# The sum of a softmax taken from ScalarE's accumulator output instead of a VectorE reduction

## The chip, the cores and the metric

The kernel runs on one core of a Trainium2 chip, as one launch. The metric is the device time of the whole launch in microseconds (us). A core has five engines, each with a queue of its own that it works through in order: TensorE (PE in the profile, with PEld for its weight loads), VectorE (DVE), ScalarE (ACT), GpSimd (POOL) and SyncE (SP, which here only starts DMAs). They meet through semaphores. Matrix products are written to a memory of their own, PSUM, which PE fills and ACT and DVE read out.

## What is computed

The input x is 8 x 512 x 128 (batch, position, feature), in float32. A first block adds the layer-normed result of a causal linear attention. The second block, in which the change lies, is a transformer of six layers over the same 8 x 512 positions: each layer has an attention over windows of 32 positions with 16 heads of 64 features, and a feed-forward part with a gated GELU. The attention of a window, cut to what matters here:

```python
sim = jnp.einsum('bhwie,bhwje->bhwij', bq, bk2) * QK_SCALE   # 32 queries x 64 keys
sim = jnp.where(mask, -jnp.finfo(sim.dtype).max, sim)
attn = jax.nn.softmax(sim, -1)
out = jnp.einsum('bhwij,bhwje->bhwie', attn, bv2)
```

The 64 keys of a window are those of the window before it and its own. Each row's softmax needs the largest score, the exponentials, and the sum of the 64 exponentials.

## The kernel before

A unit of work is a tile of 128 positions (four windows) of one batch item in one layer: 6 layers x 8 items x 4 tiles j = 192 units. The loop over t at the end of `sandwich_kernel` takes the units as a pipeline written out by hand: at step t it projects unit t, turns the queries and keys of unit t-1 to features and forms its scores, weighs the values of unit t-2, and projects the output of unit t-3. After the fourth tile of an item come the feed-forward parts: `feed_norm`, `feed_first`, `feed_middle` and `feed_last`, in the steps after it.

The loop stands in a `manual_schedule` of PE alone: PE's instructions are issued in the order in which the program writes them. The order on ACT, DVE and POOL is worked out when the kernel is built, from dependencies and priorities; a block under `tc.high_priority()` goes ahead of other ready work, and `issue_behind` ties one instruction behind another on its engine (here, each exponential behind the table load that it needs: GELU uses another table than the exponential and logarithm, so ACT loads tables twice for each batch item of a layer).

What a step does around the change, in PE's order:

- `proj` (L421) makes q and then k of unit t, in a PSUM buffer "mm". DVE multiplies by the rotary tables (L429 twice, L436 once), ACT squares both halves (L444). Only after these is the buffer free. There are two "mm" buffers, for q, k and `values` (L481), so L481 takes the one that q had. DVE sums the squares (L457).
- Between q and k, `out_project` (L603) does its products for unit t-3, which DVE adds to the state (L608).
- `by_keys` (transposes at L70, in two halves of four) turns the exponentials of unit t-2 for use as weights; ACT copies each half to pT (L564).
- `values` (L481) and ACT's copy of them (L482, and two DMA shifts for windows) follow, then `by_features` (L70, copies at L514), `weigh_values` (L574) with DVE's division by the sum (L582), and `by_features` again.
- `scores` (L527 lays down the mask, L534 adds the products) fills a PSUM tile of 128 rows x 16 heads x 64 keys. DVE takes the negated maximum of each head (L542). ACT makes 16 exponentials (L546), one for each head, 64 elements wide on 128 partitions, since each has another maximum as its bias. DVE sums all 16 x 64 in one reduction (L552) and takes the reciprocal (L553).
- `out_by_features` (L70, copies to oT at L596) ends the step.

The reduction and the reciprocal write "su", a tile of 128 x 16, of which there are two, as there are of "pe", the exponentials.

Of the kernel before, what the change touches and what calls it, by code (L numbers as in the profile page):

```python
# [8 lines left out]
F32 = mybir.dt.float32  # L9
BF16 = mybir.dt.bfloat16  # L10
AF = mybir.ActivationFunctionType
ALU = mybir.AluOpType
AX = mybir.AxisListType
PSUM = bass.MemoryType.PSUM

P = 128
# [10 lines left out]
def sandwich_kernel(ctx: ExitStack, tc: tile.TileContext, ins: dict, out: bass.AP):  # L27
    nc = tc.nc
# [57 lines left out]
    def issue_behind(later, earlier):  # L86
        tc.add_manual_dep(
            later.ins, earlier.ins.name,
            mybir.DependencyInfo(mybir.DependencyClass.NoSync, mybir.DependencyReason.DATA),
            reason="order on an engine",  # L90
        )
# [30 lines left out]
    f2 = ctx.enter_context(tc.tile_pool(name="f2", bufs=2))  # L122
# [4 lines left out]
    NP = H // 2  # L127
# [391 lines left out]
    def scores(u):  # L519

        qT, kT = u["qT"], u["kT"]


        mk = mask0 if u["j"] == 0 else mask
        sp = psum.tile([P, 2, NP, 2 * W], F32, tag="s", name="sp", bufs=1)
        for p in range(2):
            nc.tensor.matmul(  # L527
                sp[:, p], identb, mk.unsqueeze(1).to_broadcast([P, NP, 2 * W]),
                start=True, stop=False, skip_group_check=True,
            )  # L530
        for pair in range(NP):
            for w in range(4):
                for p in range(2):
                    nc.tensor.matmul(  # L534
                        sp[W * w : W * (w + 1), p, pair, :],
                        qT[HD * p : HD * (p + 1), pair, W * w : W * (w + 1)],
                        kT[HD * p : HD * (p + 1), pair, W * w : W * (w + 2)],
                        start=False, stop=True, skip_group_check=True,
                    )
        mx = f2.tile([P, 2, NP], F32, tag="mx", name="mx")  # L540
        with tc.high_priority():
            nc.vector.tensor_reduce(mx, sp, AX.X, ALU.max, negate=True)  # L542
        pe = f2.tile([P, NP, 2, 2 * W], F32, tag="pe", name="pe")
        for pair in range(NP):
            for p in range(2):
                ex = nc.scalar.activation(  # L546
                    pe[:, pair, p, :], sp[:, p, pair, :], AF.Exp, bias=mx[:, p, pair : pair + 1]
                )
                issue_behind(ex, tables[-1])
        exps.append(ex)  # L550
        su = f2.tile([P, NP, 2], F32, tag="su", name="su")
        nc.vector.tensor_reduce(su, pe, AX.X, ALU.add)  # L552
        nc.vector.reciprocal(su, su)  # L553
        u["pe"], u["su"] = pe, su

# [138 lines left out]
    with tc.manual_schedule(engines={mybir.EngineType.PE}):  # L694
# [8 lines left out]
        for t in range(len(units) + 7):  # L703
# [31 lines left out]
            if gelus:  # L735
                at(t, 0, unit_length)
            at(t, 6, feed_last, ends=True)
            at(t, 1, scores)
            at(t, 2, out_by_features)

# [90 lines left out]
```

## Time and profile before

| | |
|---|---|
| median of 3 runs | 3899.76 us (3896.29 to 3900.25) |
| the profiled execution | 3893.85 us, of which its span is 3892.1 us |
| granted TensorE clock | 0.99 |
| mean of one exponential, L546 | 376 ns, 3072 of them, 651.4 us of ACT |
| mean of one sum, L552 | 1220 ns, 192 of them, 234.2 us of DVE |
| mean of one reciprocal, L553 | 243 ns, 192 of them |
| mean of one square, L444 | 610 ns, 768 of them |
| one maximum, L542 | 1222 ns, 192 of them |

The profile lists, for each group of instructions, its source line and engine, what it writes and reads ("pe<-sp,mx"), the shapes, how often it ran, its busy time in us and the mean of one in ns, and the idle time of the engine just before it with what ended that idle time. ACT's durations overlap: the next instruction starts before the one before has ended. In the timeline every row has its start, its length, the engine, the line, and in brackets the idle time ahead of it and the releaser. "issue" is time in which an engine waited for nothing that the profile shows. The chain is followed back from the last instruction of the program to what released each, so that its shares say where a shorter instruction would have brought the end nearer.

### The profile page before, as it was taken

The numbers are of one execution on the slowest core, as the hardware profiler recorded it, in microseconds if no ns is written. First come the engines' busy times: TensorE is split into PE (matmuls) and PEld (weight loads), VectorE is DVE, ScalarE is ACT, GpSimd is POOL, SyncE is SP. The second block draws the span as 40 slices with busy tenths as digits, with TensorE's granted clock in tenths as the row PEclk, the third lists the DMA queues.
The fourth block names the chain that finished last, engine by engine and source line by source line (L and its number), as shares of the span: only waits on it lengthen the run. The fifth ranks groups of instructions, "written<-read, shape, count | busy, mean of one in ns | idle before, by whom it ended". The sixth has DMA issues, their size and how long they took to land.

```text
span 3892.1 us, 149565 instructions
## 1 busy us (share of the span) xinstructions
PE 3729.8 (96%) x65600; PEld 2474.2 (64%) x65600; DVE 2818.2 (72%) x4300; ACT 2657.5 (68%) x6745; POOL 1837.0 (47%) x1311
## 2 busy tenths in 40 slices
PE   8999989999999999999999999999999999999997
PEld 4555456666666666666666666666666666666665
DVE  4555567777867777777777777777787777777775
ACT  5565656776767777777777677777677777766664
POOL 0000025555555555555555555555555555555552
PEclk9999999999999999999999999999999999999998
DMA  2000012222222222222222322223222222222221
GB/s 81 17 9 12 6 50 71 59 66 60 76 74 63 63 63 66 71 75 65 60 62 64 82 65 66 65 56 82 70 66 59 66 65 56 65 68 68 64 67 37
DMA packets 153208, 233.46 MB, mean 60 GB/s; under 512 B 32622, under 2 KB 53356, under 8 KB 151788
## 3 DMA queue, kind: packets, MB, share of 16 engines
q1 hardware_dynamic: 152556, 223.89, 22.4%
q8 instruction: 517, 8.47, 0.9%
q14 instruction: 135, 1.11, 0.1%
HBM read 24.54 MB, written 4.19 MB: 7 GB/s over the span
## 4 chain that ended last, share of the span: by engine, by line
PE 89%; ACT 5%; issue 3%; DVE 2%; DMA 0%; POOL 0%; POOLq 0%; DVEq 0%; SPq 0%; ACTq 0%
PE tr L70 17%; PE mm L421 17%; PE mm L481 9%; PE py L603 9%; PE sp L534 7%; PE po L574 6%; PE y L282 4%; PE mm L625 3%; PE py L657 3%; PE mm L626 3%; PE sc L252 2%; PE sp L527 2%; ACT sq L444 2%; PE vv L230 2%; PE po L318 2%
## 5 line engine op out<-in xcount | busy, mean ns | idle before, releaser
L454 POOL TENSOR_TENSOR qk<-t,t 128x1024 f32<-128x1024 f32 x384 | 909.2, 2368 | 999.6 <-DVE t L436 999.5
L421 PE MATMUL mm<-wqkv,state 128*128 128x512 f32 x1536 | 727.1, 596 | 3.7 <-ACT v L482 2.6
L470 POOL TENSOR_TENSOR qk<-qk,ss 128x1024 f32<-128x1024 f32 x384 | 722.3, 1902 | 16.0
L429 DVE TENSOR_TENSOR t<-mm,tab 128x512 f32<-128x512 f32 x768 | 497.8, 685 | 242.8 <-PE mm L421 231.3
L546 ACT ACTIVATE pe<-sp,mx 128x64 f32<-128x64 f32 x3072 | 651.4, 376 | 27.6 <-DVE mx L542 27.3
L436 DVE TENSOR_TENSOR t<-mm,tab 128x1024 f32<-128x1024 f32 x384 | 465.9, 1213 | 0.0
L457 DVE TENSOR_REDUCE ss<-sq 128x16 f32<-128x1024 f32 x384 | 461.9, 1203 | 2.0 <-ACT sq L444 2.0
L444 ACT ACTIVATE sq<-mm 128x512 f32<-128x512 f32 x768 | 422.6, 610 | 47.2 <-DVE t L436 45.6
L603 PEld LDWEIGHTS py<-oT,wo 128*128 128x128 f32 x3072 | 374.8, 193 | 93.5 <-issue 56.2
L70 PEld LDWEIGHTS tr<-ident,qk 128*128 128x128 f32 x3072 | 345.7, 141 | 127.1 <-issue 105.7
L70 PE MATMUL tr<-ident,qk 128*128 128x128 f32 x3072 | 412.1, 277 | 7.4 <-ACT qT L514 2.3
L596 ACT COPY oT<-tr 128x512 f32<-128x512 f32 x384 | 207.3, 589 | 266.2 <-PE tr L70 265.2
L421 PEld LDWEIGHTS mm<-wqkv,state 128*128 128x128 f32 x1536 | 264.1, 192 | 191.6 <-issue 188.0
L481 PE MATMUL mm<-wqkv,state 128*128 128x512 f32 x768 | 367.9, 602 | 16.8 <-ACT sq L444 16.8
L603 PE MATMUL py<-oT,wo 128*128 128x128 f32 x3072 | 376.0, 276 | 1.0 <-ACT oT L596 0.9
L582 DVE TENSOR_TENSOR on<-po,su 128x1024 f32<-128x1024 f32 x192 | 235.1, 1224 | 170.1 <-PE po L574 170.1
L534 PEld LDWEIGHTS sp<-kT,qT 64*32 64x32 f32 x24576 | 271.9, 106 | 116.7 <-issue 113.8
L574 PE MATMUL po<-v,pT 64*32 64x64 f32 x24576 | 299.3, 225 | 44.7 <-issue 44.7
L482 ACT COPY v<-mm 128x1024 f32<-128x1024 f32 x192 | 194.5, 1013 | 211.0 <-PE mm L481 211.0
L534 PE MATMUL sp<-kT,qT 64*32 64x64 f32 x24576 | 312.2, 227 | 26.0 <-issue 25.2
L574 PEld LDWEIGHTS po<-v,pT 64*32 64x32 f32 x24576 | 258.5, 105 | 86.4 <-issue 86.2
L542 DVE TENSOR_REDUCE mx<-sp 128x16 f32<-128x1024 f32 x192 | 234.6, 1222 | 106.9 <-PE sp L534 106.3
(108 smaller groups left out, 5171.0 us busy)
## 6 DMA issues: line engine op xcount, KB each, us to landing
v<-v SPq DMA_DIRECT2D x1152, 128.0 KB
v<-v SPq DMA_DIRECT2D x672, 64.0 KB
wqkv<-in_L_ffn_Wqkv_dram SPq DMA_DIRECT2D x6, 1536.0 KB
wo<-in_L_ffn_Wo_dram SPq DMA_DIRECT2D x6, 512.0 KB
xin<-_attn_hidden_states_dram SPq DMA_DIRECT2D x8, 256.0 KB
xr<-_attn_hidden_states_dram SPq DMA_DIRECT2D x8, 256.0 KB
x<-xr SPq DMA_DIRECT2D x8, 256.0 KB
xr<-x SPq DMA_DIRECT2D x8, 256.0 KB
```

Of the source, the lines that this page charges most:

```text
L70: nc.tensor.transpose(ps[:cols, :rows], src, ident[:rows, :rows])
L421: nc.tensor.matmul(ps[:, a].rearrange("p h d -> p (h d)"), lhs, wqkv[:, s, a, :], start=True, stop=True)
L429: nc.vector.tensor_tensor(t2[:, a], ps[:, 1 - a], tab[:, 2 * s + 1, j, HF * a : HF * (a + 1)].unsqueeze(1).to_broadcast([P, H, HF]), ALU.mult,
L436: nc.vector.tensor_tensor(t1, ps, tab[:, 2 * s, j, :].rearrange("p (a d) -> p a d", a=2).unsqueeze(2) .to_broadcast([P, 2, H, HF]), ALU.mult,)
L444: nc.scalar.activation(sq[:, :, a, :], ps[:, a], AF.Square)
L454: nc.gpsimd.tensor_tensor(qk[:, s].rearrange("p h a d -> p a h d"), t1, t2, ALU.add)
L470: nc.gpsimd.tensor_tensor(t, t, ss[:, i, :].unsqueeze(2).to_broadcast([P, H, HD]), ALU.mult)
L481: nc.tensor.matmul(ps[:, p, :], lhs, L["wqkv"][:, 2, p, :], start=True, stop=True)
L534: nc.tensor.matmul(sp[W * w : W * (w + 1), p, pair, :], qT[HD * p : HD * (p + 1), pair, W * w : W * (w + 1)], kT[HD * p : HD * (p + 1), pa ...
L546: ex = nc.scalar.activation(pe[:, pair, p, :], sp[:, p, pair, :], AF.Exp, bias=mx[:, p, pair : pair + 1])
L574: nc.tensor.matmul(po[W * w : W * (w + 1), p, pair, :], pT[r, pair, W * w : W * (w + 1)], v2[r, w, HD * pair : HD * (pair + 1)], start=Tru ...
L603: nc.tensor.matmul(py, L["wo"][:, c, :], oT[:, c, :], start=(c == 0), stop=(c == NP - 1))
```

## The change

Each of the 16 exponentials also writes the sum of what it has computed, into its own element of "su", by ACT's accumulator output. The tile "su" is therefore made ahead of the exponentials, and the reduction on DVE is gone. The reciprocal stays.

```diff
         pe = f2.tile([P, NP, 2, 2 * W], F32, tag="pe", name="pe")
+        su = f2.tile([P, NP, 2], F32, tag="su", name="su")
         for pair in range(NP):
             for p in range(2):
                 ex = nc.scalar.activation(
-                    pe[:, pair, p, :], sp[:, p, pair, :], AF.Exp, bias=mx[:, p, pair : pair + 1]
+                    pe[:, pair, p, :], sp[:, p, pair, :], AF.Exp, bias=mx[:, p, pair : pair + 1],
+                    accum_out=su[:, pair, p : p + 1],
                 )
                 issue_behind(ex, tables[-1])
         exps.append(ex)
-        su = f2.tile([P, NP, 2], F32, tag="su", name="su")
-        nc.vector.tensor_reduce(su, pe, AX.X, ALU.add)
         nc.vector.reciprocal(su, su)
         u["pe"], u["su"] = pe, su
```

## The prediction

> **What bounds the kernel now.** I read the page first (busy shares, the chain that ended last), then the costliest groups for the lines of the change, then who waits for the exponentials, then three stretches of the timeline.
>
> ```profile
> PE 3729.8 (96%) x65600; PEld 2474.2 (64%) x65600; DVE 2818.2 (72%) x4300; ACT 2657.5 (68%) x6745; POOL 1837.0 (47%) x1311
> ...
> PE 89%; ACT 5%; issue 3%; DVE 2%; DMA 0%; POOL 0%; POOLq 0%; DVEq 0%; SPq 0%; ACTq 0%
> ```
>
> PE works through its fixed order almost without a break, and 89% of the chain is PE. ACT is on the chain for 5%, DVE for 2%. So DVE time is worth little, and ACT time costs something wherever PE stands close behind ACT.
>
> ```profile
> L546 ACT ACTIVATE pe<-sp,mx 128x64 f32<-128x64 f32 x3072 | 651.4, 376 | 27.6 <-DVE mx L542 27.3
> ...
> L552 DVE TENSOR_REDUCE su<-pe 128x16 f32<-128x1024 f32 x192 | 234.2, 1220 | 9.5 <-ACT pe L546 3.5
> ...
> L553 DVE RECIPROCAL su<-su 128x16 f32<-128x16 f32 x192 | 46.6, 243 | 0.1
> ```
>
> These are the groups of the change: 16 exponentials, one sum and one reciprocal in each of 192 steps. The sum, 234.2 us of DVE, hardly ever waited for ACT (3.5 us).
>
> ```profile
> 2051.60 3.40 ACT L546 ACTIVATE pe<-sp,mx 128x64 f32<-128x64 f32 x16
> ...
> 2055.38 1.09 ACT L444 ACTIVATE sq<-mm 128x512 f32<-128x512 f32 x2 [0.39 <-DVE t L436]
> ...
> 2055.82 1.22 DVE L552 TENSOR_REDUCE su<-pe 128x16 f32<-128x1024 f32 x1
> ...
> 2056.74 1.08 ACT L564 COPY pT<-tr 128x512 f32<-128x512 f32 x2 [0.27 <-PE tr L70]
> 2056.87 0.30 PEld L481 LDWEIGHTS mm<-wqkv,state 128*128 128x128 f32 x2
> ...
> 2058.08 0.24 DVE L553 RECIPROCAL su<-su 128x16 f32<-128x16 f32 x1
> ...
> 2058.36 1.29 DVE L429 TENSOR_TENSOR t<-mm,tab 128x512 f32<-128x512 f32 x2
> ```
>
> An ordinary step in the timeline (start, length, engine). The exponentials end at 2055.00. Behind them in ACT's queue stand the two squares of q (L444), 1.09 us; when these are done, the "mm" buffer of q is free and PE may start the values (L481). ACT idled 0.39 us, and after the squares ended at 2056.47 another 0.40 passed until PE came, at 2056.87: 1.87 us from the last exponential to L481.
>
> ```profile
> 2030.48 3.39 ACT L546 ACTIVATE pe<-sp,mx 128x64 f32<-128x64 f32 x16
> ...
> 2033.89 1.28 ACT L82 ACT_TABLE_LOAD   x1
> ...
> 2035.19 1.09 ACT L444 ACTIVATE sq<-mm 128x512 f32<-128x512 f32 x2
> ...
> 2036.33 0.30 PEld L481 LDWEIGHTS mm<-wqkv,state 128*128 128x128 f32 x2 [0.55 <-ACT sq L444]
> ```
>
> A step with the GELU table: the load stands between, ACT has no gap, and PE's L481 already waits for ACT. Every ns more on ACT here is a ns of the end.
>
> ```profile
> 2698.66 3.38 ACT L546 ACTIVATE pe<-sp,mx 128x64 f32<-128x64 f32 x16 [0.64 <-DVE mx L542]
> 2701.82 1.21 ACT L444 ACTIVATE sq<-mm 128x512 f32<-128x512 f32 x2
> 2703.04 1.07 ACT L564 COPY pT<-tr 128x512 f32<-128x512 f32 x2
> ```
>
> A third kind: the exponentials waited for the maximum, the squares follow without a gap, and L481 starts at 2703.17, 1.13 us after the last exponential.
>
> **What the Trainium skill says.** "ScalarE: Activation LUTs", section What ACT_TABLE_LOAD costs, prices an ACTIVATE at 186 ns + 0.833 ns per element, 93 more for a pointer operand, with 93 of overlap back to back: for 64 elements and a pointer bias 333 ns alone, 240 in a row. The trace has 376 for one, and (3.38 - 0.376) / 15 = 200 from start to start; the page is off by some 40 each way. Its table load of 1283 ns agrees exactly. "ScalarE activation tables: per-element evaluation and per-set limits", section What a function is on this engine, says that the accumulator output adds the results along the free dimension, but not what reading it out costs. "VectorE: DVE Perf Modes", section Two Vector instructions with no wait between them, says of VectorE that an op which also writes out its accumulator is two instructions, the second a read of the accumulator. I expect the same of ACT; no run here shows it yet.
>
> **The change part by part.**
>
> *Removed:* 192 sums, 192 x 1.220 = 234 us of DVE. They lie between other DVE work while PE does L70 and L481. The reciprocal (0.24) stays and now needs only ACT; its result is used by L582, 3 us later. What is queued behind it on DVE is the k half's L429; should the reciprocal wait for a late last sum, L429 waits too, but it already starts at 2058.36 behind 1.22 us of work that is gone. With the sum gone, k's L429 and L436 can end 1.2 us sooner, and so k's squares. That helps where PE waits for a copy queued behind those squares: the transposes of xn waited 22.5 us for the qT copy (L514). Bounds: nothing, up to about 100 us (these 22.5 and DVE's 2% of the chain, 78). I take 15, two thirds of the 22.5, since L481 and other ACT work still stand in front.
>
> *Added:* 3072 accumulator reads. I estimate one at the page's price for a one-element ACTIVATE without pointer: 187 ns of record, less 93 of overlap, 94 in a row. Bounds: below, nothing (the sum is written by the exponential itself); above, no overlap at all, (376 + 187) - 200 = 363 ns. At 94 the exponentials of a step end X = 16 x 0.094 = 1.50 us later.
>
> *What hides X.* The soonest that L481 follows the last exponential is 1.05 us (two squares and a signal), or 2.45 with a table load. I took the real interval in every step of the timeline. By tile j of the exponentials the medians are 1.88, 1.16, 2.45 and 1.87 us; the mean slack, interval less soonest, is 0.84, 0.26, 0.04 and 0.82 us (j = 0 to 3). PE is in order, so what exceeds the slack delays everything behind L481, the next scores, maximum and exponentials included: it comes back in every step. Four steps: (1.50 - 0.84) + (1.50 - 0.26) + (1.50 - 0.04) + (1.50 - 0.82) = 4.04 us; times 48 such fours, 194 us. The transposes of pe (L70) have more room: each needs only two of the exponentials, and the eighth loads about 1.6 us after the last one ends.
>
> *Moved:* nothing by hand, but only PE's order is written out; ACT's is found at build time. The first step of the timeline shows what may happen when exponentials are late:
>
> ```profile
> 572.65 0.64 ACT L546 ACTIVATE pe<-sp,mx 128x64 f32<-128x64 f32 x2
> 573.06 0.72 ACT L444 ACTIVATE sq<-mm 128x512 f32<-128x512 f32 x1
> 573.71 0.58 ACT L564 COPY pT<-tr 128x512 f32<-128x512 f32 x1
> 574.20 0.60 ACT L444 ACTIVATE sq<-mm 128x512 f32<-128x512 f32 x1
> ...
> 574.85 0.50 PEld L481 LDWEIGHTS mm<-wqkv,state 128*128 128x128 f32 x2 [1.37 <-ACT sq L444]
> ```
>
> One pT copy came before the last two exponentials, the other between the squares, and L481 waited 1.37 us. A pT copy in front of the squares costs 0.49 us (start to start). Bounds: nothing to 192 x 0.49 = 94. I take half, 47. The stalls that the chain calls "issue" (3%, 117 us) could shrink while PE waits anyway; I take nothing for that.
>
> *Sum:* 194 + 47 - 15 = +226. On the span 3892.1 that gives 4118; the profiled execution took 3893.85, 1.75 more than its span, and the median of the runs shown, 3899.76, is 5.9 above that: 4126 us.
>
> **Rivals.**
>
> *The read doesn't overlap* (25%). If the record's whole 187 ns adds to each exponential, X = 3.0 and the step costs (12.0 - 1.96) x 48 = 482, some 4380 us; at 363 ns, X = 5.8 and 4920. For it: a read has to wait until the last element has come through. Against it: the exponentials themselves start 176 ns before their predecessors end.
>
> *The read is nearly free and hides in the slack* (10%). At 47 ns X = 0.75: only j = 1 and 2 pay, (0.49 + 0.71) x 48 = 58, less 15 of relief, about 3943.
>
> *DVE's relief wins* (10%): the other side. The accumulator comes with the ACTIVATE or within 20 ns of it, X is 0.3 at most and costs (0.04 + 0.26) x 48 = 14 us, while k's squares move up, PE meets them done at xn and elsewhere, and 15 to 100 us go: about 3870. It decides below 20 ns a read for the small relief, below about 60 ns (X = 1.0, 97 us) for the greatest. For it: DVE's 2% and ACT's 5% of the chain. Against it: the sum lay where PE was busy.
>
> *The change doesn't do what it says:* the sums could still be late for L582, as the reciprocal waits for the last read. L582 starts after PE's L574, 3 us on, so this costs nothing unless X passes 3; it is within the first rival.
>
> **How the numbers follow.** The forecast, reads of 60 to 140 ns, has 55% and reaches from about 4020 to 4270. The range 3940 to 4500 adds the small-cost case and that part of the first rival with reads up to some 215 ns (15 of its 25%); left out are the relief (10%) and reads above that (10%). What a measurement of this kernel tells from no change is 0.2%, 8 us. Faster: the relief rival less a little, 9%. Within 0.2%: 3%, from the border of the two cheap cases. Slower: 88%.
>
> **What would show it.** Right: ACT has 3072 more short records at L546, the exponentials of a step last 4.9 us instead of 3.39, ACT's busy share rises beyond 75%, DVE loses 234 us, and L481 waits for ACT sq L444 in all four kinds of step, with ACT's share of the chain well above 5%. Wrong: exponentials that still last 3.4 us, or a longer stretch that ends in no wait of PE.

## The result

The changed kernel takes 4153.5 us (median of 4 runs, 4148.75 to 4155.69) beside 3898.03 us for the kernel before on the same chip: a ratio of 1.0656, 95% interval 1.0637 to 1.0674. It is slower by 255 us. In the two profiled executions the span went from 3892.1 to 4153.8 us, 262 more.

The page of the changed kernel, busy shares and the chain that ended last:

```profile
PE 3823.4 (92%) x65600; PEld 2500.1 (60%) x65600; DVE 2607.5 (63%) x4108; ACT 2910.4 (70%) x9817; POOL 1843.5 (44%) x1311
...
PE 52%; ACT 39%; DVE 6%; issue 2%; DMA 0%; SPq 0%; POOL 0%; POOLq 0%; DVEq 0%; ACTq 0%
...
L547 ACT ACTIVATE pe<-sp,mx 128x64 f32<-128x64 f32 x3072 | 913.4, 364 | 22.4 <-DVE mx L542 21.8
L547 ACT ACTIVATION_READ_ACCUMULATOR pe<-sp,mx 128x1 f32 x3072 | 789.1, 258 | 0.0
```

ACT is busy for only 70% of the span, 68% before, and still it carries 39% of the chain, 5% before. DVE lost 211 us of busy time, and its share of the chain rose from 2% to 6%. What sets the end is how late ACT is at one place, not how full it is. The 3072 new rows are the accumulator reads; each stands in the trace for 258 ns on average.

The stretch behind the exponentials of an ordinary step, in the timeline of the changed kernel:

```profile
2104.93 0.41 ACT L547 ACTIVATE pe<-sp,mx 128x64 f32<-128x64 f32 x1
...
2105.22 0.42 ACT L547 ACTIVATE pe<-sp,mx 128x64 f32<-128x64 f32 x1
2105.41 0.32 ACT L547 ACTIVATION_READ_ACCUMULATOR pe<-sp,mx 128x1 f32 x1
2105.51 1.20 ACT L444 ACTIVATE sq<-mm 128x512 f32<-128x512 f32 x2
...
2106.75 0.30 PEld L481 LDWEIGHTS mm<-wqkv,state 128*128 128x128 f32 x2 [0.58 <-ACT sq L444]
```

From one exponential to the next it is now 0.29 us, 0.20 before: a read adds 0.09 us, though its own row lasts 0.21 to 0.32 in this step, since the rows overlap. The first exponential of this step starts at 2100.88, so all 16 take 4.85 us in place of 3.39. The squares (L444) follow without the gap of 0.39 us that stood there before, and the weight load of L481 waits for them.

The step with the GELU table is another matter. In the kernel before, ACT copied to pT behind the squares (those at 2035.19 in the prediction's second timeline):

```profile
2036.16 1.08 ACT L564 COPY pT<-tr 128x512 f32<-128x512 f32 x2
```

In the changed kernel, first ACT, then PE:

```profile
2007.31 1.28 ACT L82 ACT_TABLE_LOAD   x1
2008.60 1.07 ACT L564 COPY pT<-tr 128x512 f32<-128x512 f32 x2
2009.56 2.09 ACT L444 ACTIVATE sq<-mm 128x512 f32<-128x512 f32 x4
```

```profile
2010.72 3.00 PE L481 MATMUL mm<-wqkv,state 128*128 128x512 f32 x4 [2.74 <-ACT sq L444]
```

Both pT copies (L564) now stand ahead of the squares, and PE waits 2.74 us. Then something else happens: the four matmuls of L481 take 3.00 us, while they take 1.98 in the ordinary step. The view by stretches, whose seventh number (PEclk) is the granted TensorE clock:

```profile
2006.90:2010.70 3.80, 1.08 (x9) 0.80 (x7) 2.67 (x4) 3.77 (x10) 2.25 (x2) 1.00 0.00 0
2010.70:2014.70 4.00, 3.98 (x10) 2.24 (x11) 1.22 (x1) 1.89 (x4) 1.76 (x1) 0.61 0.00 0
```

(The numbers after the stretch are its length, the busy times of PE, PEld, DVE, ACT and POOL with their counts, the clock, and DMA.) After the stall PE got 0.61 of its clock for the 4 us that follow. In 29 of the 46 such steps that I compared, the way from L481 to L574 took 4.05 to 5.42 us; in the other 17 it took 2.79, as before.

The distance from the first exponential of a step to that of the next, averaged over the steps of each kind (j is the tile of the exponentials; worked out from the timelines, the first four steps left out), is the measure for all that follows. In us:

| | j = 0 | j = 1 | j = 2 (GELU) | j = 3 |
|---|---|---|---|---|
| before | 15.73 | 15.27 | 20.26 | 17.48 |
| changed | 16.36 | 16.48 | 23.30 | 18.06 |
| squares first | 16.32 | 16.39 | 21.58 | 18.13 |
| 8 reads, squares first | 15.71 | 15.70 | 20.94 | 17.49 |
| table load later | 16.35 | 16.49 | 20.29 | 18.11 |

The differences of the first two rows, 0.63 + 1.21 + 3.04 + 0.58 = 5.46 us, times 48 give 262 us: the whole of the span's growth.

### The profile page after: what moved, and what is told of

Read it like the earlier page. It is cut to its first block, busy times and chain, and to the rows that moved or that the text cites. A ratio compares the mean times of both kernels' runs of the same rounds, so it can differ in the third digit from the quotient of the medians.

```text
span 4153.8 us, 152353 instructions
## 1 busy us (share of the span) xinstructions
PE 3823.4 (92%) x65600; PEld 2500.1 (60%) x65600; DVE 2607.5 (63%) x4108; ACT 2910.4 (70%) x9817; POOL 1843.5 (44%) x1311
## 4 chain that ended last, share of the span: by engine, by line
PE 52%; ACT 39%; DVE 6%; issue 2%; DMA 0%; SPq 0%; POOL 0%; POOLq 0%; DVEq 0%; ACTq 0%
ACT pe L547 22%; PE mm L481 10%; PE tr L70 10%; PE po L574 6%; ACT sq L444 5%; PE sp L534 4%; ACT oT L596 4%; PE y L282 4%; PE mm L625 3%; PE py L657 3%; PE mm L626 3%; PE sc L252 2%; PE vv L230 1%; ACT L76 1%; PE po L318 1%
## 5 line engine op out<-in xcount | busy, mean ns | idle before, releaser
L454 POOL TENSOR_TENSOR qk<-t,t 128x1024 f32<-128x1024 f32 x384 | 907.7, 2364 | 875.5 <-DVE t L436 875.5
L547 ACT ACTIVATE pe<-sp,mx 128x64 f32<-128x64 f32 x3072 | 913.4, 364 | 22.4 <-DVE mx L542 21.8
L547 ACT ACTIVATION_READ_ACCUMULATOR pe<-sp,mx 128x1 f32 x3072 | 789.1, 258 | 0.0
L421 PE MATMUL mm<-wqkv,state 128*128 128x512 f32 x1536 | 727.3, 596 | 4.5 <-ACT v L482 2.6
L481 PE MATMUL mm<-wqkv,state 128*128 128x512 f32 x768 | 413.8, 665 | 187.0 <-ACT sq L444 187.0
L436 DVE TENSOR_TENSOR t<-mm,tab 128x1024 f32<-128x1024 f32 x384 | 465.9, 1213 | 0.0
L70 PEld LDWEIGHTS tr<-ident,qk 128*128 128x128 f32 x3072 | 361.6, 146 | 143.0 <-issue 117.6
L444 ACT ACTIVATE sq<-mm 128x512 f32<-128x512 f32 x768 | 433.1, 658 | 5.8 <-DVE t L436 5.7
L70 PE MATMUL tr<-ident,qk 128*128 128x128 f32 x3072 | 428.2, 284 | 7.4 <-issue 2.8
L421 PEld LDWEIGHTS mm<-wqkv,state 128*128 128x128 f32 x1536 | 263.8, 192 | 192.9 <-issue 189.3
L481 PEld LDWEIGHTS mm<-wqkv,state 128*128 128x128 f32 x768 | 136.2, 197 | 331.2 <-ACT sq L444 231.9
L574 PE MATMUL po<-v,pT 64*32 64x64 f32 x24576 | 298.4, 227 | 27.8 <-issue 27.6
```

The lines of the kernel that those rows point to most:

```text
L70: nc.tensor.transpose(ps[:cols, :rows], src, ident[:rows, :rows])
L421: nc.tensor.matmul(ps[:, a].rearrange("p h d -> p (h d)"), lhs, wqkv[:, s, a, :], start=True, stop=True)
L436: nc.vector.tensor_tensor(t1, ps, tab[:, 2 * s, j, :].rearrange("p (a d) -> p a d", a=2).unsqueeze(2) .to_broadcast([P, 2, H, HF]), ALU.mult,)
L444: nc.scalar.activation(sq[:, :, a, :], ps[:, a], AF.Square)
L454: nc.gpsimd.tensor_tensor(qk[:, s].rearrange("p h a d -> p a h d"), t1, t2, ALU.add)
L481: nc.tensor.matmul(ps[:, p, :], lhs, L["wqkv"][:, 2, p, :], start=True, stop=True)
```

## The experiments

The first four ran on one chip beside the kernel before at 3892.56 us, the next three beside 3897.68, then three beside 3889.11, the last beside 3891.57.

**The reads with the sum kept** (e1). The reads write to a spare tile; DVE sums as before.

```diff
-                    accum_out=su[:, pair, p : p + 1],
+                    accum_out=sx[:, pair, p : p + 1],
...
+        nc.vector.tensor_reduce(su, pe, AX.X, ALU.add)
         nc.vector.reciprocal(su, su)
```

> The reads go to a spare tile and DVE's sum is kept and used. If the whole loss is ACT's reads (my theory), the freed DVE time bought nothing and this takes what the changed kernel takes: 4153 us, give or take 10. If the freed DVE time paid part of the reads back (the relief of 15 to 100 us in the prediction), this is slower than the changed kernel by that much: 4170 to 4250.

Measured: 4151.8 us, a ratio of 1.067 (1.0645 to 1.0694). With 234 us more of DVE work it takes what the changed kernel takes: the two ratios to the kernel before, 1.067 and 1.0656, differ by less than either interval is wide. The loss is ACT's reads, and no part of them that could be measured is paid back by DVE's freed time.

**No sum and no reads** (e2 and e8). First the relief of DVE alone, with a `tensor_scalar` in place of sum and reciprocal:

```diff
-        nc.vector.tensor_reduce(su, pe, AX.X, ALU.add)
-        nc.vector.reciprocal(su, su)
+        nc.vector.tensor_scalar(su, pe[:, :, :, 0], 1.0, None, ALU.add)
```

> Left out: the sums altogether, by DVE and by ACT; the reciprocal is replaced by one DVE operation of the same size that adds 1 to the first exponential of each head, so it still waits for the exponentials. This is the relief of DVE alone. My theory: nothing, 3885 to 3900 us. The relief rival: 15 to 100 us below the kernel before, 3800 to 3883.

Measured: 3907.78 us, 1.0042 (1.0028 to 1.0057), 0.4% slower than before. The experiment was not what I meant it to be. By the view of the tile su, the stand-in was longer than the sum and the reciprocal together, 1.46 us, that it replaced (shortest, median and longest in ns):

```profile
L552 DVE TENSOR_SCALAR su<-pe x192: 176/2005/2018, 573.7 to 3863.8; 128x16 f32<-128x16 f32 x192
```

So it ran again with a small reduction, `nc.vector.tensor_reduce(su, pe[:, :, :, 0:2], AX.X, ALU.add)`, for both instructions:

> Again the relief of DVE alone, since the operation that took the place of the reciprocal in the first try took 2.0 us, more than the sum it replaced. Left out here: the sums and reciprocals; one small reduction over the first two exponentials of each head stands for both, with no reads on ACT. Theory: the sum on DVE was covered and its absence brings nothing, 3890 to 3905 us. Relief rival: 15 to 100 us below the kernel before.

```profile
L552 DVE TENSOR_REDUCE su<-pe x192: 185/186/190, 572.6 to 3846.7; 128x16 f32<-128x32 f32 x192
```

Measured: 3888.24 us, 0.9994 (0.9986 to 1.0002). Taking 1.46 - 0.19 us of DVE out of every step brings some 5 us at most, by the interval, and may bring nothing. The sum was covered.

**Squares first** (e3), on the changed kernel; the helper that records the squares of q is left out of the later diffs.

```diff
-            nc.scalar.activation(sq[:, :, a, :], ps[:, a], AF.Square)
+            r = nc.scalar.activation(sq[:, :, a, :], ps[:, a], AF.Square)
+            if s == 0:
+                squares_q.append(r)
...
-                nc.scalar.copy(pT[:, c : c + 4, :], ps)
+                cp = nc.scalar.copy(pT[:, c : c + 4, :], ps)
+            issue_behind(cp, squares_q[-1])
```

> The changed kernel with the pT copies tied behind the squares of q on ACT. Theory: in the step with the GELU table the two copies went ahead of the squares, which made L481 0.98 us later in 48 steps (47 us), and the longer stall let TensorE's clock fall to half in many of them (another 0.6 us a step on average, 29 us). Then this takes 4153 - 76 = 4077 us, PE's stall ahead of L481 there is 1.7 to 2.0 us instead of 2.74, and no slow matmuls follow it. If the slow matmuls have another cause than the length of the stall: 4106. If the place of the copies doesn't matter: 4153.

Measured: 4073.2 us, 1.047 (1.0452 to 1.0489). ACT's timeline in a GELU step of this run:

```profile
1978.11 1.28 ACT L82 ACT_TABLE_LOAD   x1
1979.40 1.08 ACT L444 ACTIVATE sq<-mm 128x512 f32<-128x512 f32 x2
1980.37 1.08 ACT L566 COPY pT<-tr 128x512 f32<-128x512 f32 x2
```

PE's stall ahead of L481 is 1.78 us or less in all 46 of these steps, and in none of them is the stretch behind it slow (2.78 or 2.79 us every time). The order of two copies and the slow clock behind the stall that they caused were 79 us of the loss (4151.8 us, the reads with the sum kept on the same chip, less 4073.2).

**Half the reads** (e4), with the squares first.

```diff
-                    accum_out=su[:, pair, p : p + 1],
+                    **(dict(accum_out=su[:, pair, p : p + 1]) if p == 0 else {}),
...
+        nc.vector.tensor_reduce(su[:, :, 1], pe[:, :, 1, :], AX.X, ALU.add)
         nc.vector.reciprocal(su, su)
```

> Reads at 8 of the 16 exponentials, DVE sums the other 8 heads; pT copies behind the squares as in the run before. Theory with slack: the exponentials end 0.72 us later, which hides in the steps of j = 0 and 3 (slack 0.84, 0.82) and costs 0.46 and 0.68 us in those of j = 1 and 2: 55 us, 3953. If the cost goes with the number of reads, as for an engine that bounds the kernel throughout: half of what the run with 16 reads and squares first loses, about 90 us, 3988.

Measured: 3947.99 us, 1.0149 (1.0129 to 1.0169). Half the reads cost 55 us, all of them 181. The table shows why it isn't half: j = 0 and 3 pay nothing (-0.02 and 0.01 us), j = 1 pays 0.43 and j = 2 pays 0.68, beside the 0.46 and 0.68 expected. The slack of each kind of step swallows the first part of any delay.

**The table load later** (e5 on the changed kernel, e6 on the kernel before): it is made after the projection of q and tied behind the squares of q.

```diff
         issue_behind(ld, exps[-1])
+        issue_behind(ld, squares_q[-1])
...
-            if gelus:
-                gelu_only()
             at(t, 0, proj, 0)
+            if gelus:
+                gelu_only()
```

> The changed kernel with the GELU table load tied behind the squares of q, instead of straight behind the exponentials. Theory: L481 in the GELU step then follows the exponentials as in the other steps, 1.03 us after the last one instead of 3.43; 48 x 2.4 = 115 us go, and the slow matmuls after the long stall (29 us) with them: about 4010. Rival: the load of 1283 ns only moves, makes the copy of the values (L482) and the copies behind it late by as much, and PE waits there: 4077 to 4153.

Measured: 4012.39 us, 1.0303 (1.0288 to 1.0319). The GELU step is back at 20.29 us, what it took before without any reads; the other three pay as before.

> The kernel before with the table load tied behind the squares of q. Theory: the stall of 0.55 us ahead of L481 goes in 48 steps: 26 us, 3872. Rival: given back at the copy of the values, 3890 to 3900.

Measured: 3903.34 us, 1.0014 (1.0004 to 1.0025): a miss. The waits of PE in the kernel before, and then in this one:

```profile
PE po L574 <- issue: 44.7, 62, 2.1
...
PE mm L481 <- ACT sq L444: 16.8, 46, 2.2
```

```profile
PE po L577 <- issue: 65.9, 62, 2.2
...
PE mm L484 <- ACT sq L445: 3.6, 3, 2.2
```

(Total in us, times, longest.) The wait for the squares all but went, as expected, but PE's stalls for no wait that this view shows, in the run of 128 small matmuls of `weigh_values`, grew by 21 us. Many GELU steps did get shorter (median 19.40 us instead of 19.81), others longer, up to 23.3, some with slow matmuls behind such a stall. So the gain was given back.

The times of the DMA packets in the traces tell what PE waited for. One DMA queue carries instructions (packets, MB, share), here on the page of the kernel before:

```profile
q8 instruction: 517, 8.47, 0.9%
```

That is 16 KB a packet, and one packet for about 254 of the 131,200 matmuls and weight loads of PE. From 600 us on, every one of the 96 "issue" stalls of PE in the kernel before (75.7 us in total) ends between 1.15 and 1.71 us after such a packet has landed, where only 9% of moments picked at random lie so. In the run with the later load it is the same for all 108 (101.2 us). So PE stood waiting for its next instructions, and the 25.5 us more of it are the whole of the 26 us that were to be gained. This is read from the times; no run varied the supply of instructions.

**One exponential** (e7, e9, e10, e11), the opposite of the change: less on ACT, more on DVE.

```diff
-        for pair in range(NP):
-            for p in range(2):
-                ex = nc.scalar.activation(
-                    pe[:, pair, p, :], sp[:, p, pair, :], AF.Exp, bias=mx[:, p, pair : pair + 1]
-                )
+        with tc.high_priority():
+            nc.vector.tensor_tensor(
+                pe.rearrange("t c p k -> t p c k"), sp,
+                mx.unsqueeze(3).to_broadcast([P, 2, NP, 2 * W]), ALU.add,
+            )
+        ex = nc.scalar.activation(pe, pe, AF.Exp)
```

> The kernel before with less on ACT instead of more: DVE subtracts the maxima in one operation (1.2 us) and ACT takes one exponential of 1024 elements (about 1.06 us by the row of L306) in place of 16; DVE's sum is kept. The exponentials then end about 1.3 us earlier, at the price of 235 us of DVE. If ACT between the maximum and L481 is what matters (theory): the 0.55 us of the GELU step and the waits of the pe transposes (17 us) go, 3855 to 3875. If DVE time is worth something (the relief rival read backwards): slower than before, 3910 to 3990.

Measured: 4237.1 us, 1.0878 (1.0858 to 1.0898): a bad miss. The timeline of this run:

```profile
2114.31 1.21 DVE L553 TENSOR_REDUCE su<-pe 128x16 f32<-128x1024 f32 x1
...
2115.44 0.58 DVE L609 TENSOR_TENSOR state<-py,state 64x128 f32<-64x128 f32 x2
2116.05 0.25 DVE L554 RECIPROCAL su<-su 128x16 f32<-128x16 f32 x1
2116.33 1.23 DVE L436 TENSOR_TENSOR t<-mm,tab 128x1024 f32<-128x1024 f32 x1
...
2117.93 1.11 ACT L444 ACTIVATE sq<-mm 128x512 f32<-128x512 f32 x2
...
2119.09 1.98 PE L481 MATMUL mm<-wqkv,state 128*128 128x512 f32 x4 [1.72 <-ACT sq L444]
```

The exponentials came early, and so the sum was ready early, and in the order found at build time DVE did the sum, the state's additions and the reciprocal ahead of q's L436. The squares wait for L436, and L481 for the squares: PE stood there 350.7 us in total. To test whether the sum's place is the cause, the sum was written behind the projection of q, as a step of its own (`at(t, 2, sums)` after `at(t, 0, proj, 0)`):

> The single exponential again (DVE subtracts the maxima), but the sum and the reciprocal are written behind the projection of q, so that DVE does q's rotary products before the sum. If the loss of the run with one exponential came from DVE doing the sum ahead of L436, so that q's squares and L481 were late (theory): the stall ahead of L481 goes, and with it all of the loss, 3865 to 3900. If it came from the 235 us more of DVE work as such: still near 4237, 4150 at least.

Measured: 3970.16 us, 1.0202 (1.0184 to 1.0219). This is outside what was expected: most of the loss went, but 97 us of stalls at L481 stayed, in 50 steps, where the additions to the state were still ahead of L436. Next, the table load was moved as well (e10):

> As the run before, with the table load tied behind the squares of q. Theory: with one short exponential the load ends before the squares are due anyway, so no difference to the run before, within 10 us. If the load still holds the squares up: 20 us less.

Measured: 4004.45 us, 1.028 (1.0265 to 1.0295), 34 us more rather than the same. PE's "issue" stalls at the small matmuls account for 16 us of it (42.9 after 27.0), and the lower granted clock (0.982 after 0.985) for some 12 by the two spans, an estimate; the rest is open. The last step (e11) goes back to the table load in its old place and ties the additions to the state:

```diff
+            if s == 0:
+                rotated_q.append(r)
...
-                nc.vector.tensor_tensor(sl, py[r], sl, ALU.add)
+                st = nc.vector.tensor_tensor(sl, py[r], sl, ALU.add)
+            issue_behind(st, rotated_q[-1])
```

> As the run with one exponential and the later sum, with DVE's additions to the state (L608 before) also tied behind q's rotary products. In that run the stalls ahead of L481 that are left are 50, 97 us in total, all in the step of the feed-forward norm, where DVE did the additions to the state, which wait for PE, ahead of L436. Theory: these stalls go, and the slow matmuls behind them (about 30 us): 3840 to 3880, below the kernel before. Rival: the time of the run before comes from the 235 us more of DVE work, 3950 to 3970.

Measured: 3895.08 us, 1.0008 (1.0002 to 1.0014). All but some 3 us of what the single exponential had lost is regained by the order of DVE's instructions, with the 235 us more of DVE work still there. But nothing is gained on the kernel before, against what I expected. PE's stalls at L481 fell to 4.7 us, from 16.8 in the kernel before; in return its transposes (L70) wait 22.8 us for the qT copy, 14.2 before, and 13.0 for the additions to the state, 0.3 before, and DVE has 14% of the chain, 2% before. The "issue" stalls are what they were (75.7 us from 600 us on). No version tried that computes the whole softmax beats the kernel before.

## Why the prediction came out

It said 4126 us and 4153.5 were measured. By its steps, in us of the span:

| term | predicted | found |
|---|---|---|
| later exponentials beyond the slack | 194 | 184 |
| pT copies ahead of the squares | 47 | 47 |
| DVE relief | -15 | 0 |
| the rest: slower clock of PE after the stall, less fewer "issue" stalls | - | 31 |
| sum | 226 | 262 |

- *The price of a read.* The estimate of 94 ns, from "ScalarE: Activation LUTs", section What ACT_TABLE_LOAD costs, held: 0.29 - 0.20 = 0.09 us from start to start, X = 4.85 - 3.39 = 1.46 us instead of 1.50. That it held is in part luck: the row of a read, 258 ns, is longer than the 187 I took, and its overlap, 168 ns, longer than the 93; only the difference counts, and there the two errors cancel. The page has no price for an accumulator read; the runs give it. The reason given for the first rival, that a read has to wait for the last element, doesn't show in the rows: the last read starts at 2105.41, before the row of its exponential (from 2105.22, 0.42 long) has ended.
- *The slack by kind of step.* With X = 1.46 the prediction's slacks give 0.62, 1.20, 1.42 and 0.64 us; the steps j = 0, 1 and 3 grew by 0.63, 1.21 and 0.58. For j = 2 see below. The run with 8 reads confirms the threshold itself. The 184 are these three and the 1.42 of j = 2, times 48. The 1.42 is worked out, not measured: with the squares first the step j = 2 grew by 1.32, and the four by 3.68 x 48 = 177 us.
- *The order on ACT.* The half of 94 us was a hedge, and that the 47 came out is luck: not one copy in half of all steps went ahead, but both copies, 0.98 us, in the GELU step alone, 48 times. The mechanism was named rightly and its place was not. That the copies become ready while the table loads fits the timeline, but no run shows that this is the reason.
- *The relief.* It was mis-sized, small as it was: nothing that could be measured (0.9994). The transposes of xn wait as before. The reciprocal did move: it waited 106.9 us in total for the last read, and nobody waited for it.
- *What was missing.* Behind the stall of 2.74 us PE's clock falls in most GELU steps. In that step the growth is 1.42 + 0.98 + 0.64 us; the last part is what is left of 3.04. The slow matmuls (1.60 us on average in 29 of 46 steps, so 48 us in 48 steps), less the 17 us by which PE's "issue" stalls at L574 shrank (44.7 before, 27.6 after), give the same 31, but that the two are counted right one by one is an estimate. That the slow stretch comes from the stall is shown by the run with the squares first.
- *The sum.* On the span it was 36 us short: 31 for the clock, left out, and 15 for the relief, which didn't come, less the 10 by which the first term was too high.
- *The signs.* The 3072 records, the 4.85 us of a step's exponentials and the waits at L481 in all kinds of step (191 times) came as forecast. ACT's share did not rise beyond 75% but to 70; the prediction's own numbers give only some 72% ((2657.5 + 3072 x 0.094) / 4118). DVE lost 211 us and not 234.
- *The rivals.* The read overlaps, against the first one. The cheap read was out at 90 ns. The other side, DVE's relief, would have decided below 20 to 60 ns a read; the relief was measured as some 5 us at most, so it could hardly have won at any price.

## What to carry to other kernels

Before work is moved from one engine to another, look for the place where the slowest engine stands behind each of them, and measure the slack there for every kind of step: a delay costs only what exceeds the slack, and an engine at 68% can still be the one that is late. An instruction that becomes late or early also changes what stands ahead of it and behind it in an order that is found at build time, on its engine and on others; look at that order, and tie the one instruction that PE waits for. A stall that is removed can come back at the next wait: here at PE's own instructions, or at another copy. Sixteen small accumulator reads can cost more than one reduction that nobody waits for.

## What the runs showed of the hardware

- An accumulator output on ACT is a second instruction, ACTIVATION_READ_ACCUMULATOR, 191 to 318 ns by its row and 0.09 us in a row of exponentials of 64 elements. "VectorE: DVE Perf Modes", section Two Vector instructions with no wait between them, says so of VectorE; the trace shows it of ACT.
- In the changed kernel PE's clock fell to a mean of 0.61 in the 4 us behind the stall of 2.74 us, in 29 of the 46 GELU steps, and in none of those of the run with the squares first, where the stall is 1.78 us.
- The length of a stall is not all that counts there. By the clock records of the trace, the clock is at half for stretches of 3.41 us (41 of 45 in the changed kernel; the others are longer), and all of these begin on one grid of windows of 3.41 us. Of the 46 stalls, each of the 29 with slow matmuls behind it put at least 1.99 us into one window. The other 17 lay across two windows, or were short (two of 1.72 us), so that no window got more than 1.86. Over all windows from 580 us on, the kernel before lost its full clock behind the 9 in which PE was busy for 50% or less, and kept it behind 947 with 51% or more; in the changed kernel the border lies between 45 and 55%. So a window in which PE works for less than about half of the time is enough, as these traces show it. In the kernel before, some of the falls stand behind stalls of 1.70 us at L70, shorter than the 1.78; here in the view by stretches, where PE is busy for 1.70 of 3.40 us and then has half its clock:

```profile
3427.80:3431.20 3.40, 1.70 (x8) 0.59 (x7) 1.70 (x3) 0.20 (x1) 3.02 (x3) 1.00 0.67 170
3431.20:3434.60 3.40, 3.40 (x134) 2.80 (x134) 2.77 (x13) 0.60 (x3) 1.26 (x2) 0.50 0.40 103
```

"TensorE: Matmul & The Clock Gate", Part 1: The HAM clock gate, says that the clock halves after an idle window of about 3.4 us, and that the windows run freely. The grid agrees; that the window must be idle does not, and the measurement decides.
- PE's "issue" stalls in runs of small matmuls end 1.15 to 1.71 us after a packet of instructions has landed, 96 of 96 in the kernel before: they are waits for instructions, read from the times of one run after the other, not varied by an experiment.
- The `tensor_scalar` of 16 elements in the first run without sums took 2.0 us, 176 ns at its shortest, while the reduction in its place took 186 ns always. In the trace it ends as POOL's addition ends, here at 2027.49 and 2027.46:

```profile
2025.48 2.01 DVE L552 TENSOR_SCALAR su<-pe 128x16 f32<-128x16 f32 x1
```

```profile
2025.10 2.36 POOL L454 TENSOR_TENSOR qk<-t,t 128x1024 f32<-128x1024 f32 x1 [2.02 <-DVE t L436]
```

The same holds for 190 of the 192: an addition of POOL (L454) was under way, and they end 28 to 39 ns behind it. The two that met no POOL instruction took 176 and 177 ns. "SBUF — State Buffer", section Who interferes with whom, says that a `tensor_scalar` can take ports that DVE shares with GpSimd, where whoever comes first blocks the other for its whole instruction, and that a `tensor_reduce` never contends. The trace agrees on both: the reduction met such an addition in 190 of 192 steps too, and took 185 to 190 ns.
